# Interleaving two table-filling phases, spreading their pieces, and three smaller changes in an edge-gated graph kernel

## The chip, the cores and the metric

The kernel runs on one core of one Trainium2 chip. The metric is the device time of one execution in microseconds (us). A timed comparison alternates the changed kernel with the kernel before on the same chip. Chips differ: over the jobs of this study the kernel before had medians between 1218 and 1237 us. Kernels of different jobs are therefore compared by their ratio to the kernel before in the same job, not by their times. Unless a run is called slow, every run used here was in the fast state.

PE is the matmul engine (PEld its weight load), DVE the vector engine, ACT the scalar engine, POOL is GpSimd and SP the engine that issues most plain DMAs.

## The reference

There are 16 batches of 1024 nodes with 256 features. For each edge (u, v) of a sparse adjacency matrix, a small two-layer network gives a gate. The gated and the plain neighbour sums are then projected and added to the node:

```python
pre_u = einsum('bud,dk->buk', h_t, W1[:d])
pre_v = einsum('bvd,dk->bvk', h_t, W1[d:])
hidden = relu(pre_u[:, :, None, :] + pre_v[:, None, :, :] + b1)
S = sigmoid(einsum('buvk,ko->buvo', hidden, W2)[..., 0] + b2[0])
a_t = einsum('buv,bud->bvd', S * A_a, h_t)
m_t = einsum('uv,bud->bvd', A_m, h_t) * h_t
z_t = beta1*h_t + beta2*(einsum('bvd,de->bve', a_t, Wa) + ba) \
                + beta3*(einsum('bvd,de->bve', m_t, Wm) + bm)
```

The adjacency has about 0.9% of its entries set, so the kernel works on lists of edges instead of on all pairs.

## The kernel before

The batches form 4 groups of 4, the nodes 8 row blocks of 128. That makes 32 *blocks* (group, row block), each of ten *steps*. A step handles 128 edges: GpSimd gathers 128 rows of a table (`fetched`, one half x·W1-upper, the other half x), PE expands the target side of each edge (`pc`), DVE computes the gate, ACT the sigmoid and the weights (`left`), and PE aggregates into `acc`.

```python
def expand(n):                       # PE: target side of each edge of step n
    pcs[n] = psc.tile([P, GD], FP, name="pc")            # two buffers in PSUM
    for h in range(2):
        nc.tensor.matmul(pcs[n][:, c], marks[..], cuts[k][:, w, c], ...)
def gate(n):                         # DVE, then ACT
    nc.vector.tensor_tensor(t, fetched[..], pcs.pop(n), ALU.add)
    for b in range(GB):
        nc.vector.scalar_tensor_tensor(t[:, b, :], ..., accum_out=sc[:, b:b + 1])
    nc.scalar.activation(gt, sc, AF.Sigmoid, bias=b2_b)
    ...                              # left = one-hot x value x gate, on ACT
```

Beside this main line runs side work. `rows` fills a gather table ahead of need (products with `w_u`, in two halves per row block; all products of a half go into a buffer of the two-deep PSUM pool "misc"). `halves` prepares the next block's target side X (products with `w_v`; the rounding rest `low` is moved to the other 64 partitions by a swap matmul). `block_end` computes the output products, and `lists` makes the edge lists, on DVE above all.

```python
def rows(k, tab=None):
    for h in range(2):
        step = yield                                     # one piece per step
        half_product(p, hTs[k], w_u, h, False)           # 8 matmuls into "misc"
        nc.scalar.copy(tab[:, c], p)
def halves(k):
    ...                                                  # X[:, 0] and low, two pieces
    for h in range(2):
        yield
        nc.tensor.matmul(pl, swap, low[:, c], start=True, stop=True)
        for w in range(NW):
            s = slice((1 - w) * W, (2 - w) * W)
            nc.scalar.copy(X[s, w, c], pl[s])
# the main loop, cut
for n in range(total + 2):
    k, s = divmod(n, T)
    aggregate(n - 1); fetch(n - 1 + NF); gate(n)
    do(n)                                                # postponed DVE work, h_blk add too
    ...                                                  # s in 3..6: output products of block k-1
    if k + 1 < BS and s in (0, 2, 3, 4, 7): go(parts, n)     # a piece of halves
    if n in loads: load_hT(loads[n])                     # 512 KB of x transposed
    if n in at:    go(piece, n)                          # a piece of rows
    if n + 2 < total: expand(n + 2)
```

Groups 0 and 1 take turns every four row blocks, so that each edge list serves both. Their table pieces are packed tightly in the early blocks, and groups 2 and 3 have theirs in steps 8 and 9 of most blocks, with a cluster of group 3 in blocks 21 and 22.

## Time and profile before

| | kernel before |
|---|---|
| time, median of 3 runs | 1236.83 us (1234.14 to 1241.36) |
| span of the profiled run, mean granted clock | 1225.1 us, 0.964 |
| first gate starts at | 78.1 us |
| blocks 0 to 9 | 414.1 us |
| blocks 10 to 23 | 463.1 us, 33.1 a block |
| blocks 24 to 30 | 220.7 us, 31.5 a block |
| block 31 with the tail | 49.1 us |

The stretches are cut at the start of the gate's first DVE instruction in every tenth step, so they add up to the span. The profiled run was faster than all three timed ones. Differences between profiles therefore understate the change by several us against the timed runs, and the two sums below are not expected to agree.

Two more lines are needed later. These are ACT's instructions just before the first gate, from the timeline of the kernel before (start, us, engine, line, operation, tiles, shape, count, and in brackets the idle time before it and what ended it).

```profile
73.11 0.73 ACT L300 CAST few<-made 128x640 uint8<-128x640 f32 x1 [5.70 <-DVE made L294]
73.84 2.36 ACT L431 CAST X<-misc 64x512 fp32r<-64x512 f32 x4
76.10 0.72 ACT L523 CAST mark<-whose 128x640 fp32r<-128x640 uint8 x1
```

ACT took its instructions in the order of the program here. The four copies behind the swap matmuls (2.36 us) stand between the last list copy and the `mark` that the first expansion needs.

### The profile page before, as it was taken

What the parts mean: (1) busy time and instruction counts of PE and PEld (TensorE: products, weight loads), DVE (VectorE), ACT (ScalarE), POOL (GpSimd) and SP (SyncE); (2) the same over time, 40 slices, a digit from 0 to 9 for tenths busy, and PEclk for the clock granted to TensorE, in tenths of its full rate; (3) what the DMA queues carried; (4) which work ended last, traced back from release to release, by engine and by line L of the source; (5) the groups of instructions that cost most, each with busy time, mean ns of one, the idle gap of its engine ahead of it and who ended that gap; (6) DMA issues with size and microseconds to landing.
All of it is one profiled execution on the core that took longest, in us unless ns stands there. A gap on an engine that the chain in (4) does not pass through costs nothing. (4 is left out here: it accounts for less than half of the span.)

```text
span 1225.1 us, 23939 instructions
## 1 busy us (share of the span) xinstructions
PE 1110.8 (91%) x7697; PEld 723.6 (59%) x7697; DVE 1068.5 (87%) x3517; ACT 844.0 (69%) x2562; POOL 416.3 (34%) x412
## 2 busy tenths in 40 slices
PE   7665989988888988999999999999999999999986
PEld 6543666645555655666666556666666655665553
DVE  7667868898997889899999999998888999999994
ACT  2245567766666756778777777777777777887763
POOL 0345562326244314423233333332222333333330
PEclk9777999989898989999999999999999999999998
DMA  9688899977889979899999999999998998999992
GB/s 285 221 296 296 268 321 330 335 262 237 315 291 332 353 295 343 323 356 362 356 363 375 351 355 325 347 351 394 387 358 322 353 322 315 329 339 329 325 334 97
DMA packets 151975, 393.50 MB, mean 321 GB/s; under 512 B 16816, under 2 KB 110512, under 8 KB 115632
## 3 DMA queue, kind: packets, MB, share of 16 engines
q0 software_dynamic: 49504, 299.85, 66.5%
q1 hardware_dynamic: 85776, 77.08, 19.5%
q10 hardware_dynamic: 16560, 14.95, 3.8%
q8 instruction: 63, 1.03, 0.3%
q14 instruction: 72, 0.59, 0.1%
HBM read 395.88 MB, written 50.33 MB: 364 GB/s over the span
## 5 line engine op out<-in xcount | busy, mean ns | idle before, releaser
L459 POOL DMA_INDIRECT fetched<-table,uidx x320 | 326.7, 1021 | 717.1 <-PE acc L567 525.5
L550 DVE SCALAR_TENSOR_TENSOR t<-t,w_b 128x256 f32<-128x256 f32 x1280 | 469.6, 422 | 19.8
L546 DVE TENSOR_TENSOR t<-fetched,pc 128x1024 f32<-128x1024 f32 x320 | 389.2, 1216 | 68.9 <-PE pc L530 38.9
L567 PE MATMUL acc<-fetched,left 128*32 128x256 f32 x4096 | 323.4, 393 | 28.1 <-ACT left L556 21.9
L556 ACT ACTIVATE left<-left,gt 128x32 f32<-128x32 f32 (+1 forms) x1280 | 300.3, 306 | 10.4
L530 PE MATMUL pc<-X,mark 128*128 128x512 f32 x640 | 249.8, 472 | 5.4 <-ACT mark L523 5.4
L567 PEld LDWEIGHTS acc<-fetched,left 128*32 128x32 f32 x4096 | 121.3, 110 | 195.6 <-issue 71.6
L553 ACT ACTIVATE gt<-sc,b_b 128x4 f32<-128x4 f32 x320 | 95.5, 299 | 158.8 <-DVE t L550 150.7
L385 PE MATMUL misc<-w_u,hT 128*128 128x256 f32 x512 | 132.7, 407 | 19.8 <-ACT fetched L401 8.4
L530 PEld LDWEIGHTS pc<-X,mark 128*128 128x128 f32 x640 | 120.0, 195 | 29.8 <-ACT mark L523 5.9
L615 PE MATMUL misc<-w_m,LT 128*128 128x256 f32 x496 | 133.7, 392 | 0.0
L615 PE MATMUL misc<-w_a,LT 128*128 128x256 f32 x496 | 127.3, 379 | 0.0
L385 PEld LDWEIGHTS misc<-w_u,hT 128*128 128x128 f32 x512 | 99.3, 203 | 43.9 <-ACT fetched L401 8.9
L385 PE MATMUL misc<-w_v,hT 128*128 128x256 f32 x512 | 122.6, 383 | 0.0
L540 ACT ACTIVATE left<-onehot,val 128x128 f32<-128x128 bf16 (+1 forms) x320 | 117.5, 367 | 0.0
L615 PEld LDWEIGHTS misc<-w_m,LT 128*128 128x128 f32 x496 | 88.9, 189 | 34.8 <-issue 25.5
L385 PEld LDWEIGHTS misc<-w_v,hT 128*128 128x128 f32 x512 | 98.3, 192 | 13.2
L343 POOL DMA_INDIRECT val<-in_adjT_dram,vidx x80 | 85.3, 1066 | 60.9 <-DVE b_p L194 33.4
L550 DVE DVE_READ_ACCUMULATOR t<-t,w_b 128x1 f32 x1280 | 104.0, 81 | 0.0
L575 ACT COPY ev<-acc 128x512 f32<-128x512 f32 x128 | 74.9, 585 | 41.6 <-PE acc L567 28.6
L615 PEld LDWEIGHTS misc<-w_a,LT 128*128 128x128 f32 x496 | 94.2, 190 | 12.8
L585 PE MATMUL misc<-ident,ev 128*128 128x128 f32 x512 | 81.0, 289 | 15.8 <-DVE h_blk L619 8.5
(140 smaller groups left out, 820.3 us busy)
## 6 DMA issues: line engine op xcount, KB each, us to landing
hT<-in_xT_dram SPq DMA_DIRECT2D x40, 512.0 KB
h_blk<-in_x_dram SPq DMA_DIRECT2D x31, 512.0 KB
out_dram<-h_blk SPq DMA_DIRECT2D x31, 512.0 KB
table<-tab SPq DMA_DIRECT2D x26, 512.0 KB
table<-in_x_dram ACTq DMA_DIRECT2D x24, 512.0 KB
fetched<-table,uidx POOLq DMA_INDIRECT x320
table<-in_x_dram SPq DMA_DIRECT2D x8, 512.0 KB
table<-fetched SPq DMA_DIRECT2D x6, 512.0 KB
```

What stands on the lines that cost most here:

```text
L343: nc.gpsimd.indirect_dma_start(out=val[:, i, j:j + 1], out_offset=None, in_=adj_flat, in_offset=bass.IndirectOffsetOnAxis(ap=vidx[:, i, j: ...
L385: nc.tensor.matmul(p[:, bb * D:(bb + 1) * D], hT[:, 2 * h + bb, i, :], wt[:, i, :], start=(i == 0 and not begun), stop=(i == DC - 1), skip ...
L459: nc.gpsimd.indirect_dma_start(out=fetched[n % NF], out_offset=None, in_=table[g], in_offset=bass.IndirectOffsetOnAxis(ap=uidx[:, vt * NW ...
L530: nc.tensor.matmul(pcs[n][:, c], marks[n // TW][:, j * P:(j + 1) * P], cuts[k][:, w, c], start=True, stop=True)
L540: nc.scalar.activation(lefts[n][:, :m, :, 0, :], onehot[:, i, o:o + m, :].unsqueeze(2).to_broadcast([P, m, GB, V]), AF.Copy, scale=val[:, ...
L546: nc.vector.tensor_tensor(t, fetched[n % NF][:, :GD].rearrange("p (b d) -> p b d", b=GB), pcs.pop(n).rearrange("p (b d) -> p b d", b=GB), ...
L550: nc.vector.scalar_tensor_tensor(t[:, b, :], t[:, b, :], 0.0, w2_b, ALU.max, ALU.mult, accum_out=sc[:, b:b + 1])
L553: nc.scalar.activation(gt, sc, AF.Sigmoid, bias=b2_b)
L556: nc.scalar.activation(lefts[n][:, :m, b, 1, :], lefts[n][:, :m, b, 0, :], AF.Copy, scale=gt[:, b:b + 1])
L567: nc.tensor.matmul(accs[h][b * 2 * V:(b + 1) * 2 * V, r, :], left[:, i, b].rearrange("p k v -> p (k v)"), f[:, GD + b * D:GD + (b + 1) * D ...
L585: nc.tensor.transpose(pt[:, i * P:(i + 1) * P], ev[:, r, c * P:(c + 1) * P], ident)
L615: nc.tensor.matmul(pz[:, bb * D:(bb + 1) * D], LTs[k][:, c, 2 * h + bb, i, :], wt[:, c, :], start=False, stop=(i == 1 and c == DC - 1), sk ...
```

## The change

The intent is to interleave stretches bound by different engines, and to take waits and work off PE. The parts, with numbers used below: (a) the swap matmul goes, ACT copies `low` across the partitions itself. (b) The expansion for step n+2 comes right after the aggregation instead of at the end of the step. (c) Groups 0 and 1 take turns every six row blocks, and the `rows` pieces are spread evenly by `plan`. (d) GpSimd instead of ACT issues the small copies of the first four lists. With (c) come a new start-up script, an earlier fifth list, a pool of three for the reloaded x, and one buffer instead of two for the list tile `made`; no run separates these from the turns.

```diff
-        for h in range(2):
+        for w in range(NW):
             yield
-            c = slice(2 * h * D, (2 * h + 2) * D)
-            pl = small("pl")
-            nc.tensor.matmul(pl, swap, low[:, c], start=True, stop=True)
-            for w in range(NW):
-                s = slice((1 - w) * W, (2 - w) * W)
-                nc.scalar.copy(X[s, w, c], pl[s])
+            nc.scalar.copy(X[(1 - w) * W:(2 - w) * W, w, :], low[w * W:(w + 1) * W].bitcast(FP))
...
-                nc.scalar.dma_start(whose[...], few[...])
+                (nc.gpsimd if vt < EARLY else nc.scalar).dma_start(whose[...], few[...])
...
-    order = [(g, vt) for h in range(2) for g in range(2) for vt in range(h * NT // 2, (h + 1) * NT // 2)]
+    FIRST = 6
+    order = [(g, vt) for some in (range(FIRST), range(FIRST, NT)) for g in range(2) for vt in some]
...
-    at.update(zip((10 * i + s for i in range(7, 15) for s in (8, 9)), ((2, vt) ...)))
-    at.update(zip((178, 179, 188, 189, 198, 199, 208, 209, 211, 215, 217, 218, 219, 221, 228, 229), ((3, vt) ...)))
+    # plan: (load, first piece, second piece) in steps
+    plan(turn[NT:], ((0, 5, 8), (6, 12, 15), (12, 18, 22), (17, 25, 28), (24, 32, 35), (31, 38, 42), (38, 45, 48), (43, 50, 52)))
+    plan([(2, vt) ...], ((62 + 10 * i, 68 + 10 * i, 73 + 10 * i) for i in range(NT)))
+    plan([(3, vt) ...], ((146, 152, 157), (156, 162, 167), *((153 + 10 * i, 158 + 10 * i, 161 + 10 * i) for i in range(2, NT))))
+    plan(again, ((103,), (113,), (125,), (133,)))
...
         do(n)
+        if n + 2 < total:
+            expand(n + 2)
...
-        if k + 1 < BS and s in (0, 2, 3, 4, 7):
+        if k + 1 < BS and s in (0, 2, 3, 4, 6):
...
-        if n + 2 < total:
-            expand(n + 2)
```

More of the change, by code (lines that the diff above doesn't have):

```diff
@@ L178 @@
         nc.vector.tensor_scalar(slot_of[:, w, :], upto[:, :TW], float(P), row, ALU.mult, ALU.add)
-    swap = fixed([P, P], "swap", FR)
-    for w in range(NW):
-        nc.vector.tensor_scalar(swap[:, w * W:(w + 1) * W], upto[:, (1 - w) * W:(2 - w) * W], row, None, ALU.is_equal)
     ident = fixed([P, P], "ident")
@@ L216 @@
     hts = main.enter_context(tc.tile_pool(name="hts", bufs=NT + 2))
+    hta = main.enter_context(tc.tile_pool(name="hta", bufs=3))
     wk = main.enter_context(tc.tile_pool(name="wk", bufs=3))
@@ L288, in lists @@
         yield
-        mark = big.tile([P, E], FP, name="made")
+        mark = big.tile([P, E], FP, name="made", bufs=1)
         nc.vector.tensor_scalar(mark, slot, R[:, 0:1], None, ALU.is_lt)
@@ L305, in lists @@
             for h in range(2):
-                nc.scalar.dma_start(whose[h * W:(h + 1) * W, vt * NW + w, :], few[w * W:(w + 1) * W])
+                (nc.gpsimd if vt < EARLY else nc.scalar).dma_start(whose[h * W:(h + 1) * W, vt * NW + w, :], few[w * W:(w + 1) * W])
         pe = aside(vt)
@@ L361, in after @@
         due.setdefault(step, []).append(f)
-    order = [(g, vt) for h in range(2) for g in range(2) for vt in range(h * NT // 2, (h + 1) * NT // 2)]
-    again = [(g, vt) for g, vt in order if vt >= NT // 2]
+    FIRST = 6
+    order = [(g, vt) for some in (range(FIRST), range(FIRST, NT)) for g in range(2) for vt in some]
+    again = [(g, vt) for g, vt in order if vt >= FIRST]
     order += [(g, vt) for g in range(2, NG) for vt in range(NT)]
@@ L372, in load_hT @@
         g, nt = k
-        hTs[k] = hts.tile([P, GB, DC, P], FP, name="hT")
+        hTs[k] = hta.tile([P, GB, DC, P], FP, name="hT_") if k in again else hts.tile([P, GB, DC, P], FP, name="hT")
         nc.sync.dma_start(hTs[k].rearrange("p b c n -> p (b c) n"),
@@ L423, in halves @@
         nc.scalar.copy(X[W:, 1, :], X[W:, 0, :].bitcast(FP))
-        for h in range(2):
+        for w in range(NW):
             yield
-            c = slice(2 * h * D, (2 * h + 2) * D)
-            pl = small("pl")
-            nc.tensor.matmul(pl, swap, low[:, c], start=True, stop=True)
-            for w in range(NW):
-                s = slice((1 - w) * W, (2 - w) * W)
-                nc.scalar.copy(X[s, w, c], pl[s])
+            nc.scalar.copy(X[(1 - w) * W:(2 - w) * W, w, :], low[w * W:(w + 1) * W].bitcast(FP))
     engines = mybir.EngineType
@@ L465 @@
     made = [lists(vt) for vt in range(NT)]
-    turn = [order[i] for i in (*range(2 * NT // 2, 3 * NT // 2), *range(NT // 2))]
-    turn += [(1, vt) for _, vt in turn]
+    turn = [(g, vt) for g in range(2) for vt in (*range(FIRST, NT), *range(FIRST))]
     tabs = [fetched[0][:, :GD], *(f[:, GD:] for f in fetched)]
@@ L477 @@
         copy_h(turn[i], nc.sync)
-    script = ("r 0 0", "r r 0", "r 1", "0 r 1 1", "0 0 r r", "1 r 0 2 2", "r 0 0 v 2", "1 1 r r 2",
-              "r 1 r 3 3", "1 1 2 2 r h", "2 r r h 3", "2 2 3 h", "3 3 f h h")
+    script = ("r 0 0", "r r 0", "r 1", "0 r 1 1", "0 0 r r", "1 r 0 2 2", "r r 0 0 v 2", "1 1 r r",
+              "2 r 1 r", "2 2 r r 1 1 h", "2 h 3 3", "2 2 h 3", "f h h 3", "3 3")
     m = 0
@@ L666, with plan @@
     advance = {0: (3,), 2: (3,), 4: (3,)}
-    for i, n in zip(range(EARLY, NT), (0, 30, 50, 80)):
+    for i, n in zip(range(EARLY, NT), (0, 20, 50, 80)):
         for o in (0, 4, 5, 6, 7, 9, 11, 13, 15, 17):
             advance[n + o] = (*advance.get(n + o, ()), i)
-    loads = dict(zip((0, 1, 2, 6, 9, 13, 17, 23), turn[NT:]))
-    at = dict(zip((3, 5, 7, 8, 9, 11, 15, 17, 18, 19, 21, 25, 27, 28, 29, 31), (k for k in turn[NT:] for _ in range(2))))
-    loads.update(zip((58, 64, 66, 68, 70, 72, 93, 103), again))
-    loads.update(zip((74, 80, 86, 90, 113, 123, 133, 143), ((2, vt) for vt in range(NT))))
-    at.update(zip((10 * i + s for i in range(7, 15) for s in (8, 9)), ((2, vt) for vt in range(NT) for _ in range(2))))
-    loads.update(zip((173, 183, 193, 203, 206, 209, 214, 223), ((3, vt) for vt in range(NT))))
-    at.update(zip((178, 179, 188, 189, 198, 199, 208, 209, 211, 215, 217, 218, 219, 221, 228, 229),
-                  ((3, vt) for vt in range(NT) for _ in range(2))))
-    begun = set(turn)
+    loads, at = {}, {}
+    def plan(blocks, ns):
+        for k, (load, *pieces) in zip(blocks, ns):
+            loads[load] = k
+            at.update((n, k) for n in pieces)
+    plan(turn[NT:], ((0, 5, 8), (6, 12, 15), (12, 18, 22), (17, 25, 28), (24, 32, 35), (31, 38, 42), (38, 45, 48),
+                     (43, 50, 52)))
+    plan([(2, vt) for vt in range(NT)], ((62 + 10 * i, 68 + 10 * i, 73 + 10 * i) for i in range(NT)))
+    plan([(3, vt) for vt in range(NT)], ((146, 152, 157), (156, 162, 167), *((153 + 10 * i, 158 + 10 * i, 161 + 10 * i)
+                                                                             for i in range(2, NT))))
+    plan(again, ((103,), (113,), (125,), (133,)))
+    begun = set(turn[:NT])
     end = parts = piece = last = None
@@ L749 @@
             load_hT(loads[n])
-            if loads[n] not in begun or n < 30:
+            if loads[n] not in begun:
                 copy_h(loads[n])
+                begun.add(loads[n])
         if n in at:
```

## The prediction

> **What bounds the kernel now.** I read the page first: its busy shares and its slices, then the waits, then stretches of ten steps each. A step is one gather of 128 rows, its gate and its aggregation; ten make a block, and 32 blocks the kernel.
>
> ```profile
> PE 1110.8 (91%) x7697; PEld 723.6 (59%) x7697; DVE 1068.5 (87%) x3517; ACT 844.0 (69%) x2562; POOL 416.3 (34%) x412
> PE   7665989988888988999999999999999999999986
> DVE  7667868898997889899999999998888999999994
> PEclk9777999989898989999999999999999999999998
> ```
>
> PE and DVE are both nearly full, and neither is full all the time: the first 40% of the slices are thinner on both and have a lower granted clock, and in slices 28 to 31 DVE thins while PE does not. So one has to ask which is ahead in which stretch. The gate's first instruction (t<-fetched,pc) starts each step on DVE; I took its start times from the trace as the borders of the blocks. Here are blocks 0 to 4, 12, 21, 22 and 27. Columns: us, then busy us (instructions) of PE, weight load, DVE, ACT, POOL; granted clock; DMA share; GB/s.
>
> ```profile
> 78.10:131.30 53.20, 39.46 (x220) 25.80 (x220) 37.35 (x134) 26.64 (x81) 25.30 (x25) 0.77 0.86 295
> 131.30:175.00 43.70, 39.09 (x256) 27.16 (x258) 38.03 (x124) 27.47 (x80) 30.50 (x30) 1.00 0.96 318
> 175.00:215.10 40.10, 38.32 (x262) 26.01 (x266) 30.49 (x96) 27.46 (x83) 13.60 (x14) 1.00 0.94 326
> 215.10:256.70 41.60, 37.87 (x261) 24.02 (x261) 36.55 (x127) 28.48 (x88) 10.69 (x11) 0.88 0.85 301
> 256.70:295.00 38.30, 33.01 (x217) 20.39 (x216) 35.11 (x116) 24.14 (x73) 16.50 (x16) 0.96 0.83 284
> 557.00:589.50 32.50, 32.04 (x238) 21.00 (x234) 30.19 (x96) 25.70 (x80) 10.09 (x10) 1.00 0.97 366
> 850.20:887.90 37.70, 37.46 (x262) 25.61 (x261) 30.44 (x97) 27.49 (x84) 9.92 (x10) 1.00 1.02 379
> 887.90:921.90 34.00, 33.76 (x246) 22.56 (x247) 30.49 (x96) 26.33 (x81) 9.92 (x10) 1.00 0.99 357
> 1050.80:1081.90 31.10, 30.21 (x219) 18.88 (x218) 30.11 (x96) 24.64 (x78) 10.15 (x10) 1.00 0.90 325
> ```
>
> And blocks 2, 12 and 21 with w_u's instructions alone, PE and weight load only (x times W1's upper half, which fills the gather tables ahead of need):
>
> ```profile
> 175.00:215.10 40.10, 9.77 (x40) 7.27 (x40) 1.00 0.94 326
> 557.00:589.50 32.50, 3.89 (x16) 2.88 (x16) 1.00 0.97 366
> 850.20:887.90 37.70, 9.71 (x40) 7.27 (x40) 1.00 1.02 379
> ```
>
> What to see: a block without w_u and without list making takes 31.1 us and DVE works 30.1 of it: that is the floor, set by DVE. Eight w_u records are one half of a table's row block. A block with 2 halves takes 32.5, with 3 (x24) 34.0, with 5 (x40) 37.7; there PE has 0.2 to 0.5 us idle and DVE up to 7. The line through 2 and 5 halves is 29.05 + 1.73 per half, and gives 34.2 for 3. PE sets those blocks. Making the edge lists costs DVE about 6.4 and 5.0 us more in the two blocks that one list spans (36.5 and 35.1 against 30.1), and those blocks take 38 to 42.
>
> ```profile
> DVE t L546 <- PE pc L530: 38.9, 31, 5.7
> ACT X L431 <- PE misc L428: 20.2, 28, 1.5
> PEld misc L389 <- ACT X L431: 18.2, 23, 1.5
> PEld misc L428 <- ACT LT L588: 18.0, 24, 2.0
> DVE t L546 <- DMA fetched<-table,uidx: 11.5, 14, 2.4
> ```
>
> The gate waits for PE's expansion (pc), hardly for the gathers; and the swap matmul (L428) both waits for and holds up a buffer of the two-deep "misc" PSUM pool.
>
> **What the Trainium skill says.** "Perfetto Trace Analysis", section "Optimization Strategy": where the most-contended engine changes over time, interleaving the regimes can help. The blocks above are that case: PE-bound ones (5 halves) lie beside DVE-bound ones (none). "TensorE: Matmul & The Clock Gate", section "Wait — 56ns, not 53.3ns?": matmuls start N over 2.4 GHz plus about 2.5 ns apart, 215.7 ns for 512 columns. The trace differs: the 512-column fp32r swap holds its successor 0.42 us, the 256-column fp32 records start 0.216 us apart, so I take 0.42. Same page, "What's actually happening": an idle window halves the clock; here the clock is 0.77 in block 0 and 0.88 to 0.96 where PE idles 3 to 7 us of 40, so idle costs twice there. "DMA: Bandwidth & Descriptors", "Issuing engines are not separate DMA queues": another issuing queue saves only issue time. That bounds the copies moved from ACT to GpSimd: four ACT issues took 2.64 us at 47.3 us.
>
> **The change part by part.** (a) Swap removed. 64 matmuls go, 2 per block: 2 × 0.42 = 0.84 us of PE, and with them most of the wait at L389 and of those at the swap itself, (18.2 + 18.0) / 32 = 1.1 us per block on the weight-load side, of which I count half. PE per block: 29.05 − 1.4 = 27.65, plus 1.73 per half. ACT trades four copies of 0.58 (2.33) for two of 64x1024, which L423 shows to take 1.05 (2.09): no gain worth counting. With 2 halves PE then needs 31.1, just DVE's floor; with 3 it needs 32.8.
> (b) Expansion of step n+2 right after the aggregation, ahead of the side work. PE does the same work, but the pc waits (38.9 us, of which three steps of block 0 have 12.8) should nearly go from the other blocks. This makes it possible to reach the floor; I do not count it twice.
> (c) Turns of six blocks and even spreading. From the schedule, halves per block before: 5, 5, 5, 1 in blocks 0 to 3; 2 each in 7 to 14 and in 17 to 20, then 5 and 3 in 21 and 22. After: 2, 3, 3, 3, 3, 2 in blocks 0 to 5; about 2 in 7 to 13; 2 or 1 in 15 to 23. Four instead of eight 512 KB reloads of x transposed go too: 2 MB of 393, hidden.
> (d) 16 small list copies to GpSimd, 10.6 us of ACT issue in the start-up, where ACT is half idle.
>
> Sum. Blocks 10 to 23 took 463.1 us (492.2 to 955.3). PE and DVE now both stand at 31.1, so I take 31.3: 14 × 31.3 = 438.2, gain 25. Blocks 24 to 30 took 220.7; 7 × 31.2 = 218.4, gain 2. Early blocks, 0 to 9, took 414.1. Block 0: three halves fewer by plan, cold clock, 53.2 to 48. Block 1: 43.7 to 40.5 (DVE 38 plus 2.5 of waits). Blocks 2 and 3: list 5 moves in by ten steps beside 3 halves; 81.7 to 78.5. Block 4: no list now, 3 halves on PE, 38.3 to 34. Blocks 5 to 9, list-bound: 197.2 to 192. Together 393, gain 21. Start-up before the first gate (78.1) and tail (49.1): the same chains; 0. Total 48, so 1237 − 48 = 1189; two for gathers that come under pressure at a faster pace: 1191.
>
> **The rivals.** First, gathers become the bound. For: DMA share 0.97 to 1.02 in the w_u blocks; block 12's 366 GB/s over 32.5 us would become 380 at 31.3. Against: block 21 ran at 379 with share 1.02 and its gates waited for PE, not DMA; all gather waits are 11.5 us. If true, blocks 10 to 23 stay near 32.3: 14 us of gain lost, 1205. Second, the early expansion stalls PE: it needs the buffer that gate n empties, and where 2 to 4 us of list work stand ahead of that gate on DVE, PE waits instead of doing side work. For: blocks 3 to 9 have such list work. Against: PE has slack there and side work is needed a step later. If true, early gain shrinks to about 5: 1207. Third, DVE's floor is the bound everywhere and the clustering was already paid inside PE slack: then only blocks 18 to 23 and block 0 gain, 1215. Fourth, the moved copies stand ahead of the first gathers on GpSimd and delay the start by 3 to 8 us.
>
> **Range and chances.** The late gain (18 to 30) is read from a fitted line, the early one (5 to 35) is rough, start-up ±5. In the middle 1191, eighty per cent within 1172 to 1213. The 2% limit is 1212, so faster 0.86, same 0.13, slower 0.01.
>
> **What would show it.** Blocks 10 to 30 should all take 31 to 31.6 us, DVE busy 30.1, PE busy under it; no L428; pc waits under 15 us; blocks 1 to 4 between 34 and 41. Gates waiting over 30 us for gathers would show the first rival; PE waits for DVE t before pc the second; a first gate after 82 us the fourth. Blocks of 32.5 with 2 halves would disprove (a).

## The result, and the profile after

| | before | after |
|---|---|---|
| median, 4 runs each | 1235.49 us (1232.73 to 1241.36) | 1198.01 us (1196.87 to 1204.65) |
| ratio of fast runs, 95% interval | | 0.9702 (0.965 to 0.9753): faster |
| profiled span, clock | 1225.1 us, 0.964 | 1195.2 us, 0.973 |

A ratio here is the mean time of one kernel's fast runs over that of the other's fast runs of the same rounds, so it is not quite the ratio of the medians. The change gains 37 us; 46 were predicted. By stretches of the two profiles:

| stretch | before | after | gain | predicted gain |
|---|---|---|---|---|
| start to the first gate | 78.1 | 68.5 | 9.6 | 0 |
| block 0 | 53.2 | 43.8 | 9.4 | 5 |
| blocks 1 to 9 | 360.9 | 352.1 | 8.8 | 16 |
| blocks 10 to 23 | 463.1 | 463.3 | −0.2 | 25 |
| blocks 24 to 30 | 220.7 | 217.8 | 2.9 | 2 |
| block 31 and tail | 49.1 | 49.6 | −0.5 | 0 |

The total came out near, but its parts did not: more than half of the expected gain was to come from blocks 10 to 23, and there came none. From the page of the kernel after (busy shares, then two rows of the 40 slices, in tenths):

```profile
PE 1097.9 (92%) x7633; PEld 724.7 (61%) x7633; DVE 1066.9 (89%) x3515; ACT 840.4 (70%) x2498; POOL 426.1 (36%) x428
DVE  8769879989988988899899999999999999999994
PEclk9968899999999999999999999999999999999998
```

The thin DVE slices 28 to 31 of before are gone, and the clock drops only in a few early slices. PE ran 64 matmuls fewer, as it should. Now blocks 0, 3, 12, 13, 21 and 27 of the kernel after (columns as in the prediction's table of blocks):

```profile
68.54:112.33 43.79, 35.33 (x214) 21.92 (x213) 37.29 (x133) 25.91 (x78) 28.00 (x28) 0.79 0.80 252
198.05:236.14 38.09, 36.22 (x264) 24.90 (x256) 34.97 (x118) 26.71 (x79) 16.30 (x16) 1.00 0.89 316
532.72:565.69 32.97, 32.63 (x234) 21.74 (x235) 30.28 (x96) 25.81 (x78) 10.48 (x11) 1.00 0.98 363
565.69:601.42 35.73, 33.48 (x233) 21.66 (x231) 30.29 (x97) 25.70 (x78) 10.61 (x10) 0.95 0.97 358
830.78:862.76 31.98, 31.41 (x229) 20.52 (x227) 30.29 (x96) 25.68 (x78) 9.74 (x10) 1.00 1.00 363
1021.10:1052.21 31.11, 29.97 (x218) 19.01 (x216) 30.12 (x97) 24.57 (x76) 10.21 (x11) 1.00 0.93 329
```

Block 27 is at the floor of 31.1, as predicted. Block 21 no longer carries five halves: 37.7 became 32.0. But block 12, an ordinary block with two halves, took 32.97 where it had taken 32.50, with PE still at 32.63, although its swap matmuls are gone. Block 13 was longer still, with a clock of 0.95. The waits of the kernel after that answer to those shown of before (us in total, times, longest):

```profile
DVE h_blk L612 <- PE misc L608: 20.6, 21, 2.7
DVE low L419 <- ACT X L418: 19.7, 16, 4.4
DVE t L539 <- DMA fetched<-table,uidx: 8.6, 14, 1.2
DVE t L539 <- PE pc L523: 3.4, 3, 2.0
```

The gate's wait for PE's expansion fell from 38.9 to 3.4 us, and all waits at the swap are gone. In their place DVE waits 20.6 us for the output products (`h_blk`, once 1.3) before it can add them. This wait stands in front of the next gate on DVE's queue. ACT at the start, from the timeline of the kernel after:

```profile
65.87 0.72 ACT L298 CAST few<-made 128x640 uint8<-128x640 f32 x1 [7.03 <-DVE made L292]
66.50 0.72 ACT L516 CAST mark<-whose 128x640 fp32r<-128x640 uint8 x1
```

The last list copy came 7.2 us earlier (73.11 to 65.87), and `mark` followed it at once instead of after 2.36 us of swap copies; together that is the 9.6 us.

Block 13's loss has another cause. These are one matmul group on PE and the issue of the load that it needs:

```profile
551.09 0.65 SPq L373 DMA_DIRECT2D hT__6071<-in_xT_dram  x1
...
570.69 3.26 PE L384 MATMUL misc<-w_v,hT__6071 128*128 128x256 f32 x8 [2.25 <-DMA hT__6071<-in_xT_dram]
```

The 512 KB load was issued five steps before the w_v product that needs it and took 19.5 us to land (at 570.64). PE stood still for 2.25 us, and the granted clock was at half for the next 3.4 us: these eight matmuls took 3.26 us instead of 1.89.

### The profile page after: what moved, and what is told of

It reads as the page before. It is cut to its first block, busy times and chain, and to the rows that moved or that the text cites. A ratio compares the mean times of both kernels' runs of the same rounds, so it can differ in the third digit from the quotient of the medians.

```text
span 1195.2 us, 23788 instructions
## 1 busy us (share of the span) xinstructions
PE 1097.9 (92%) x7633; PEld 724.7 (61%) x7633; DVE 1066.9 (89%) x3515; ACT 840.4 (70%) x2498; POOL 426.1 (36%) x428
## 3 DMA queue, kind: packets, MB, share of 16 engines
q0 software_dynamic: 50016, 300.50, 68.5%
## 5 line engine op out<-in xcount | busy, mean ns | idle before, releaser
L539 DVE TENSOR_TENSOR t<-fetched,pc 128x1024 f32<-128x1024 f32 x320 | 388.8, 1215 | 22.4 <-DMA fetched<-table,uidx 8.6
L560 PE MATMUL acc<-fetched,left 128*32 128x256 f32 x4096 | 334.2, 394 | 32.3 <-ACT left L549 16.8
L523 PE MATMUL pc<-X,mark 128*128 128x512 f32 x640 | 238.1, 454 | 21.1 <-DVE t L539 13.6
L560 PEld LDWEIGHTS acc<-fetched,left 128*32 128x32 f32 x4096 | 129.9, 110 | 177.2 <-issue 46.9
L523 PEld LDWEIGHTS pc<-X,mark 128*128 128x128 f32 x640 | 97.2, 191 | 156.6 <-issue 102.2
L608 PE MATMUL misc<-w_m,LT 128*128 128x256 f32 x496 | 127.1, 378 | 0.0
L384 PE MATMUL misc<-w_u,hT 128*128 128x256 f32 x448 | 109.2, 390 | 11.0 <-ACT few L298 3.6
L384 PE MATMUL misc<-w_v,hT 128*128 128x256 f32 x448 | 107.9, 384 | 0.0
L384 PEld LDWEIGHTS misc<-w_u,hT 128*128 128x128 f32 x448 | 85.8, 195 | 27.3 <-issue 4.4
L384 PEld LDWEIGHTS misc<-w_v,hT 128*128 128x128 f32 x448 | 86.7, 194 | 14.3
L581 ACT COPY LT<-misc 128x512 f32<-128x512 f32 x128 | 71.1, 575 | 24.0 <-PE pc L523 12.0
```

The lines of the kernel that those rows point to most:

```text
L384: nc.tensor.matmul(p[:, bb * D:(bb + 1) * D], hT[:, 2 * h + bb, i, :], wt[:, i, :], start=(i == 0 and not begun), stop=(i == DC - 1), skip ...
L523: nc.tensor.matmul(pcs[n][:, c], marks[n // TW][:, j * P:(j + 1) * P], cuts[k][:, w, c], start=True, stop=True)
L539: nc.vector.tensor_tensor(t, fetched[n % NF][:, :GD].rearrange("p (b d) -> p b d", b=GB), pcs.pop(n).rearrange("p (b d) -> p b d", b=GB), ...
L560: nc.tensor.matmul(accs[h][b * 2 * V:(b + 1) * 2 * V, r, :], left[:, i, b].rearrange("p k v -> p (k v)"), f[:, GD + b * D:GD + (b + 1) * D ...
L608: nc.tensor.matmul(pz[:, bb * D:(bb + 1) * D], LTs[k][:, c, 2 * h + bb, i, :], wt[:, c, :], start=False, stop=(i == 1 and c == DC - 1), sk ...
```

## The experiments

Twelve kernels ran, in four jobs on four chips; all gave correct results. To compare blocks 10 to 23, the length of the stretch and PE's busy time in it are given each time. PE's busy time holds stalls inside a stream of matmuls too, so it is read as "the PE sequence got longer", not as pure work.

### First job: which of the parts

**late_expand**: the kernel after, with the expansion back at the end of the step.

```diff
         do(n)
-        if n + 2 < total:
-            expand(n + 2)
...
             go(piece, n)
+        if n + 2 < total:
+            expand(n + 2)
```

> The changed kernel with one edit: the expansion of step n+2 goes back to the end of the step. Theory 'order of neighbours': in the changed trace a step's matmul groups cost PE 0.309 (side work to aggregation) + 0.309 (aggregation to expansion) + 0.337 + 0.231 = 1.19 us of start-to-start time beside their own rows, in the old order 0.028 + 0.418 + 0.327 + 0.309 = 1.08, so 0.10 us a step or 1.0 us a block is given back in the PE-bound blocks. Then blocks 11 to 23 fall from 32 to 33 us to about 31.3, blocks 24 to 30 rise from 31.1 to about 31.4, and the whole gets 8 to 12 us faster than the changed kernel (about 1188). Rival 'pc waits': the late expansion is what made the gate wait for pc (38.9 us before, little now); then the waits return and the whole gets 5 to 12 us slower (about 1207).

**three_small**: the kernel before with (a), (b) and (d), without the turns and the spreading.

> The kernel before with the three small changes only: no swap matmul, expansion early in the step, list copies of the first four lists issued by GpSimd; old turns, old start-up script, old loads. Theory: the early expansion gives back in PE-bound blocks what the swap's removal gains there, so two-half blocks stay at 32 to 32.5; blocks 24 to 30 reach 31.1; start-up gains a few us from the copies. 10 to 15 us under before, about 1222; then turns and spreading are worth the other 24. Rival: the small changes are the gain and the turns nothing: about 1200.

**before_early**: the kernel before with (b) alone.

```diff
         do(n)
+        if n + 2 < total:
+            expand(n + 2)
...
-        if n + 2 < total:
-            expand(n + 2)
```

> The kernel before with the early expansion alone. 'Order of neighbours' says: PE-bound blocks 10 to 22 get about 1 us slower each (33.5 with two halves), DVE-bound blocks 24 to 30 get 0.3 faster, the early blocks lose their pc waits: within 10 us of before, more likely slower, 1235 to 1245. 'Pc waits' says 10 to 20 us faster, 1215 to 1225.

**keep_swap**: the kernel after with the swap matmul put back.

```diff
-            nc.scalar.copy(X[(1 - w) * W:(2 - w) * W, w, :], low[w * W:(w + 1) * W].bitcast(FP))
+            pl = small("pl")
+            nc.tensor.matmul(pl, swap, low[:, c], start=True, stop=True)
+            ...   # and the four copies, pieces in steps 0, 2, 3, 4, 7
```

> The changed kernel with the swap matmul put back (64 matmuls, their PSUM buffers and four half copies a block). If the swap cost PE 0.8 us a block plus half of the waits around it, as the prediction counted (1.4), the PE-bound blocks 7 to 23 and 0 to 5 rise by that: 20 to 30 us slower than the changed kernel, about 1222. If it cost only its own 0.4 us each where PE is the bound: about 12 to 16 slower, 1212. If DVE is the bound everywhere: 0 to 3.

| run | median (before: 1232.62, 15 runs) | ratio, 95% | blocks 0 to 9 | blocks 10 to 23 | PE busy in these |
|---|---|---|---|---|---|
| late_expand | 1200.42, 4 runs | 0.9734 (0.9659 to 0.9809) | 394.3 | 462.5 | 445.5 |
| three_small | 1212.03, 4 runs | 0.9839 (0.9769 to 0.991) | 404.9 | 462.8 | 451.9 |
| before_early | 1234.68, 12 runs | 1.0027 (0.9987 to 1.0068) | 413.9 | 467.5 | 460.5 |
| keep_swap | 1210.64, 4 runs | 0.9824 (0.9755 to 0.9893) | 405.5 | 462.0 | 454.4 |

The early expansion by itself gives nothing. It does what it was made for: the gate's waits for the expansion fell from 38.9 to 8.4 us. But blocks 10 to 23 became longer and PE busier. One line for that stretch of the kernel before, then the same of before_early:

```profile
492.20:955.34 463.14, 452.19 (x3263) 295.26 (x3261) 423.79 (x1348) 358.52 (x1103) 144.53 (x144) 1.00 0.97 355
```

```profile
491.15:958.66 467.51, 460.53 (x3289) 298.99 (x3288) 424.67 (x1347) 359.94 (x1107) 143.73 (x144) 1.00 0.96 352
```

PE does the same matmuls, 8.3 us longer. The starts of successive matmuls in blocks 11 to 19 and 24 to 30 show why: what a matmul costs its successor depends on the neighbours. Before, a step has the borders side work to expansion (median 0.028 us), expansion to expansion (0.418), expansion to aggregation (0.327) and aggregation to side work (0.310): 1.08 us. With the early expansion they are aggregation to expansion (0.309), expansion to expansion (0.337), expansion to side work (0.232) and side work to aggregation (0.309): 1.19 us. That is 0.10 us per step or 1.0 us per block if PE is the bound. The median of eight ordinary blocks (11 to 15 and 18 to 20) went from 32.7 to 33.2, so about half of it shows. This is what the theory "order of neighbours" had expected, a run within 10 us of before. The side work also comes later, and DVE's waits move to what hangs on it.

keep_swap against the kernel after shows (a) to be real: ratio 0.9824 against 0.9702, with intervals that just do not overlap. That is about 1.2% or 15 us, the middle case of the expectation (the swap's own 0.4 us each) and not the 20 to 30 us that 1.4 us a block would give. In blocks 10 to 23 the two profiles are alike: 462.0 and 463.3 us. three_small, 20 us under before by its ratio, fell between its theory (10 to 15) and its rival. late_expand missed both theories, between the two. PE's busy time fell by 7.3 us against the kernel after (452.8 to 445.5), as the neighbours say, but the stretch stayed at 462.5, because a new wait took the gain. The wait list of blocks 10 to 23 has this line for late_expand, against 2.7 us in the kernel after:

```profile
PEld misc L384 <- DVE low L419: 8.8, 6, 2.4
```

A w_u piece placed one step after a w_v piece wants the "misc" buffer that DVE's `low` has not read yet; this was in blocks 18 to 23, where the piece lies in step 1. three_small, finally, has ordinary blocks at 31.8 to 32.0 with one exception, where the kernel after has 32.0 to 33.2 and block 13 with 35.7. So something in the spreading makes ordinary blocks slower.

### Second job: what in the spreading

**pieces_89**: the kernel after, with the pieces of groups 2 and 3 back in steps 8 and 9 of their blocks, still spread over the blocks.

```diff
-    plan([(2, vt) ...], ((62 + 10 * i, 68 + 10 * i, 73 + 10 * i) ...))
-    plan([(3, vt) ...], ((146, 152, 157), (156, 162, 167), *((153 + 10 * i, 158 + 10 * i, 161 + 10 * i) ...)))
+    plan([(2, vt) ...], ((62 + 10 * i, 68 + 10 * i, 69 + 10 * i) ...))
+    plan([(3, vt) ...], ((146, 158, 159), (156, 168, 169), *((153 + 10 * i, 158 + 10 * i, 159 + 10 * i) ...)))
```

> The changed kernel with the two w_u pieces of a block in its steps 8 and 9 again, as before the change, instead of 8 and 3 (or 2 and 7, 8 and 1); the same number per block, the same loads. Theory 'lumps': in steps 3 to 6 PE already has the output products, and a piece there makes DVE wait for them (the h_blk additions waited 20.6 us for PE in the changed kernel, 1.3 before), the gate comes late and PE then waits at the aggregation. With the pieces at 8 and 9 the h_blk waits fall under 6 us and blocks 11, 12 and 14 to 22 fall from 32 to 33.5 to the 31.8 that the kernel with the three small changes shows with two pieces: 8 to 10 us faster than the changed kernel, about 1189. Rival: spread pieces are better for PE, and the blocks stay or rise: 0 to 5 us slower.

**early_loads**: the kernel after, with the loads of x transposed of group 2 and three of the four reloads 8 or 10 steps earlier.

```diff
-    ... ((62 + 10 * i, 68 + 10 * i, 73 + 10 * i) ...)
-    plan(again, ((103,), (113,), (125,), (133,)))
+    ... ((54 + 10 * i, 68 + 10 * i, 73 + 10 * i) ...)
+    plan(again, ((95,), (105,), (115,), (133,)))
```

> The changed kernel with the loads of x transposed for the second part of groups 0 and 1 and for group 2 issued 8 to 10 steps earlier, pieces unmoved. Theory: PE waited 2.4 us at 459.6 and 2.7 us at 570.7 for such a load, after which the clock fell to half for 3.4 us each; blocks 9, 10 and 13 (42.2, 35.6, 35.7) fall by about 2.5 each: 6 to 8 us faster than the changed kernel, about 1191. Rival: the loads are slow because the DMA engines are full, and come late anywhere: no change.

**both_moves**: both edits.

> Both: pieces at steps 8 and 9 and the earlier loads. If the two causes are separate their gains add: 14 to 18 us faster than the changed kernel, about 1182, blocks 10 to 23 in sum 445 to 450 against 463. If they are one (the load waits only happen because PE is thrown off), the gain is that of the better one alone.

**before_noswap**: the kernel before with (a) alone.

> The kernel before without the swap matmul, nothing else changed: old turns, late expansion. From the PE sequence of block 12 (swap to expansion 0.75, transposes to swap 0.51 us, the shorter second expansion matmul behind it 2 x 0.19 given back, and part of the evictions' waits) the two-half blocks should fall from 32.5 to about 31.5, under the 31.8 that they take with the early expansion. In all 10 to 16 us under before, about 1220. If the swap hid in PE waits instead: no change.

| run | median (before: 1234.8, 7 runs) | ratio, 95% | blocks 0 to 9 | blocks 10 to 23 | PE busy in these |
|---|---|---|---|---|---|
| pieces_89 | 1195.26, 4 runs (one slow, 1211.1) | 0.9667 (0.9613 to 0.9721) | 404.7 | 450.6 | 445.2 |
| early_loads | 1204.97, 4 runs | 0.976 (0.9715 to 0.9805) | 401.8 | 462.9 | 452.6 |
| both_moves | 1194.46, 4 runs | 0.9673 (0.9616 to 0.9731) | 399.6 | 455.9 | 447.4 |
| before_noswap | 1215.16, 4 runs | 0.9842 (0.9797 to 0.9886) | 407.7 | 460.3 | 447.9 |

pieces_89 tests the middle: the same early part up to step 68, the same order and the same matmuls, but 12.7 us less in blocks 10 to 23. First the mechanism in the kernel after, PE's timeline in block 12 (lines left out), then the DVE instruction that waits:

```profile
546.95 1.89 PE L384 MATMUL misc<-w_u,hT 128*128 128x256 f32 x8
548.77 1.07 PE L560 MATMUL acc<-fetched,left 128*32 128x256 f32 x16
...
550.34 1.02 PE L608 MATMUL misc<-w_m,LT 128*128 128x256 f32 x4
551.21 1.03 PE L608 MATMUL misc<-w_a,LT 128*128 128x256 f32 x4
```

```profile
552.27 0.75 DVE L612 SCALAR_TENSOR_TENSOR h_blk<-h_blk,be,misc 128x512 f32<-128x512 f32 x1 [1.28 <-PE misc L608]
```

And the same place of pieces_89:

```profile
554.75 1.07 PE L560 MATMUL acc<-fetched,left 128*32 128x256 f32 x16
...
556.32 1.02 PE L608 MATMUL misc<-w_m,LT 128*128 128x256 f32 x4
557.18 1.03 PE L608 MATMUL misc<-w_a,LT 128*128 128x256 f32 x4
```

```profile
559.13 0.74 DVE L612 SCALAR_TENSOR_TENSOR h_blk<-h_blk,be,misc 128x512 f32<-128x512 f32 x1
```

Steps 3 and 4 of a block are PE's fullest: the output products of the block before lie there. The kernel after puts a w_u piece of 1.9 us into step 3 as well. PE then ends the second set of output products at 552.2, when DVE has already stood for 1.28 us. The next gate comes behind this addition on DVE, at 552.94, and so starts late. Without the piece in step 3 PE has ended at 558.2 and DVE comes at 559.13 without a wait. In blocks 10 to 23, the wait list has these lines for three_small and for the kernel after (and none at all for pieces_89):

```profile
DVE h_blk L611 <- PE misc L607: 1.1, 2, 0.8
```

```profile
DVE h_blk L612 <- PE misc L608: 10.3, 13, 2.0
```

So 13 of the 14 blocks had it, and its size goes with the place of the piece. In blocks 10 to 17 (a piece in step 3 up to block 14, in step 2 in blocks 15 and 16) the waits come to 8.8 us and pieces_89 gains 11.4, with the same number of halves; 3.3 of these lie in block 13, where the load came almost in time in its profile. In blocks 18 to 23 (piece in step 1) the waits come to 1.5 us and the gain to 1.3.

The wait at `h_blk` is not the only form that this cost takes. late_expand has the pieces in the same steps as the kernel after, and waits in blocks 10 to 23 like this:

```profile
DVE t L539 <- PE pc L523: 9.3, 25, 0.9
DVE h_blk L612 <- PE misc L608: 2.1, 13, 0.2
```

There the gate waits for PE's expansion instead, and the stretch is as long (462.5). Moving the pieces to steps 8 and 9 with the expansion late (late_expand to mixed, of the third job) shortens blocks 10 to 17 by 6.9 us, on another chip. On one chip, early_loads and both_moves differ in the pieces alone, and the stretch fell from 462.9 to 455.9. So the place of the piece costs time under both orders, and the order of the expansion decides where DVE waits.

In the whole run the gain of pieces_89 is small (0.9667 against 0.9702, intervals overlapping; 8 to 10 us were expected). Its profile lost 8.8 us again in blocks 0 to 9 against the kernel after (404.7 to 395.9). The two programs are the same up to step 68, and 6.3 us of the difference lie in blocks 1 to 6, so most of this is scatter between runs and chips. It is also the limit of what single profiles can say about the early part.

early_loads missed. Block 13 came down from 35.7 to 32.6 us, but other waits appeared, such as one of 2.6 us at 831.84 for a load of group 3, which has the same lead of five steps and was not moved. Whether the earlier loads pushed this one back was not tested. (The wait at 459.6 that the expectation names is not put down to a load by the trace.) Both moves together gave no more than pieces_89 alone.

before_noswap settles (a) in the whole run: ratio 0.9842. Of the same eight ordinary blocks two (12 and 20) waited for a load of x in this profile; the median of the others fell by 0.6 (32.7 to 32.1; 31.5 was expected). With the early expansion on both sides (before_early to three_small) the median of the eight fell by 1.3 (33.2 to 31.9). With the spread pieces on both sides (keep_swap to the kernel after) it fell by 0.2 (33.1 to 32.8). With the swap gone, adding the early expansion and (d) (three_small) brings nothing in the whole run, and PE is 4.0 us busier in the stretch (447.9 to 451.9).

### Third job: the turns alone, the start, and a mixture

**turns_only**: the kernel before with (c) alone, that is, the kernel after with (a), (b) and (d) undone.

> The kernel before with turns of six, the new start-up script and the new loads and pieces alone: swap kept, late expansion, list copies issued by ACT. The three small changes alone gave 0.984 of before. If the parts add, turns alone give 0.970 / 0.984 = 0.986 of before, about 1217, with blocks 0 to 9 about 10 us shorter and blocks 10 to 23 no better than before (the two clustered blocks 21 and 22 gain 8, the two-half blocks lose as much by the piece beside the output products). Rival: turns are worth what I forecast (c) to give, 25 us or more, and the small changes overlap with them: 1205.

**copies_act**: the kernel after, with ACT issuing the list copies again, as before.

```diff
-                (nc.gpsimd if vt < EARLY else nc.scalar).dma_start(whose[...], few[...])
+                nc.scalar.dma_start(whose[...], few[...])
```

> The changed kernel with the list copies of the first four lists issued by ACT again. Theory: their issue time stands in ACT's in-order queue before the evictions that the start-up waits for; the kernels with GpSimd issue have their first gate at 68.5 to 73.1 us, those with ACT issue at 77.3 to 79.2. First gate 5 to 7 us later, about 75, and the whole 5 to 8 us slower than the changed kernel, about 1205. Rival: the earlier first gate comes from the new script: no change.

**mixed**: pieces_89, with the expansion late up to step 230 and early from there on, where no table is filled any more.

```diff
+        # with the pieces in steps 8 and 9
-        if n + 2 < total:
+        if n >= 230 and n + 2 < total:
             expand(n + 2)
...
+        if n < 230 and n + 2 < total:
+            expand(n + 2)
```

> The changed kernel with the w_u pieces at steps 8 and 9, and the expansion late in the step while there are w_u pieces (to step 229), early after. From the PE sequences: two-half blocks at 31.5 (late, no swap, pieces together) instead of 31.8 (early) and 32 to 33.5 (changed kernel); blocks 24 to 30 at 31.1. Blocks 10 to 23 in sum about 445, the whole about 1188, 0.992 of the changed kernel, the fastest of all. Rival: the late expansion brings the pc waits back and the two-half blocks stay at 32 or above.

| run | median (before: 1218.42, 11 runs) | ratio, 95% | first gate | block 0 | blocks 1 to 9 | blocks 10 to 23 |
|---|---|---|---|---|---|---|
| turns_only | 1199.31, 4 runs | 0.9833 (0.9804 to 0.9863) | 76.7 | 43.2 | 342.2 | 466.1 |
| copies_act | 1185.72, 4 runs | 0.9737 (0.9701 to 0.9772) | 75.0 | 42.8 | 340.4 | 458.9 |
| mixed | 1171.02, 6 runs | 0.9617 (0.9586 to 0.9647) | 71.1 | 41.0 | 338.1 | 462.8 |

This chip is faster by some 15 us for the kernel before, and copies_act, which differs from the kernel after only in who issues 16 small copies, took 340.4 us in blocks 1 to 9 instead of 352.1. The difference of the chips therefore seems to lie in the early blocks; only ratios, and the block borders common to many runs, may be compared.

Those borders are clear in two places. Over the whole study, block 0 takes 40.9 to 44.2 us in all ten kernels that have the turns of six and 48.5 to 53.2 in all four that have not. The first gate comes at 68.5 to 73.1 us where GpSimd issues the list copies and at 75.0 to 79.2 where ACT does. Three pairs of kernels agree on the way: DVE's wait in the start-up for ACT's copy to `L` (`s_of` in the wait lists) is 3.3 to 3.5 us shorter with GpSimd issuing (before to three_small 10.2 to 6.7, copies_act to the kernel after 4.7 to 1.4, turns_only to keep_swap 6.5 to 3.0; only the second pair differs in nothing else). In the whole run the copies are worth at most a little: 0.9737 against 0.9702, which the intervals do not separate.

turns_only came nearer to its theory (0.986) than to its rival of 1205, with 0.9833. mixed was the fastest so far, as expected, but blocks 10 to 23 took 462.8 us in its profile where 445 were expected. The profiled run of mixed was its slowest (1182.87, the other five 1167.57 to 1178.56). PE waited for a load of x transposed four times, once for 6.62 us. This is its line in the list of PE's waits:

```profile
PE misc L384 <- DMA hT<-in_xT_dram: 14.4, 4, 6.6
```

All four are loads of group 3 with a lead of five steps.

### Fourth job: a longer lead

**mixed_loads**: mixed, with the loads of group 3 eighteen steps ahead instead of five; three of them go into the pool of three buffers.

```diff
-    ... *((153 + 10 * i, 158 + 10 * i, 159 + 10 * i) ...)
+    ... *((140 + 10 * i, 158 + 10 * i, 159 + 10 * i) ...)
-        hTs[k] = hta.tile(...) if k in again else hts.tile(...)
+        hTs[k] = hta.tile(...) if k in again or k in ((3, 2), (3, 3), (3, 4)) else hts.tile(...)
```

> The mixed kernel (pieces at steps 8 and 9, expansion late to step 229) with the loads of x transposed for group 3 issued 18 steps ahead of their first piece instead of 5, three of them in the idle buffers of the second pool. In the trace of mixed PE waited 7.1, 2.7, 3.4 and 3.0 us for just these loads, four waits of 16 us in blocks 18 to 21, and in the kernels with the same 5-step lead 1 to 5 us there. If the lead is the cause these waits vanish, blocks 18 to 22 fall to 31.5 to 32, blocks 10 to 23 to about 446 in sum, and the ratio to before goes from mixed's 0.962 to about 0.952. If loads come late at random whatever the lead, waits of the same size stay and the ratio too.

Measured: 1169.81 us, 6 runs (1164.46 to 1174.39), beside 1219.53 for the kernel before (11 runs): ratio 0.9594 (0.9563 to 0.9625). That misses the expectation of more, but it is the fastest version of the study, and its interval is clear of the kernel after's (0.965 to 0.9753), as mixed's just is. The stretch of blocks 10 to 23:

```profile
449.73:899.41 449.68, 440.55 (x3225) 288.06 (x3223) 423.80 (x1347) 354.53 (x1076) 149.00 (x146) 1.00 1.00 371
```

PE's busy time is the lowest of all, no group-3 load is waited for any more, and there is no wait at `h_blk`. The block mean is 32.1 us all the same. The gates of this stretch now wait 10.1 us in all for their gathers (7.2 before, 6.0 after), 0.7 a block, at a DMA share of 1.00: this is the first rival of the prediction, met late and on a small scale. Against mixed the interval does not separate (0.9586 to 0.9647), so the longer lead shows in the waits and not yet in the time. How often mixed's other runs had its load waits is not known, as only the slowest was profiled. That the late expansion does better than the early one in this setting is likewise only indicated, by 4.6 us less PE busy time than in pieces_89; the stretches are as long, 449.7 and 450.6.

## Why the prediction was right or wrong

**The whole**: 1191 predicted, 1198 measured, within the range, and rightly called faster by over 2%. The nearness of the total is in part luck: 25 us failed to come in blocks 10 to 23 and 7 in blocks 1 to 9, and 14 came that were not forecast, 9.6 in the start and 4 in block 0.

**(a) The swap: right in direction, too large in size.** The step "27.65, plus 1.73 per half" meant 1.4 us less per ordinary block. They fell by 1.3 in one pair of kernels, by 0.6 from the kernel before and by 0.2 in the kernel after; PE's busy time in blocks 10 to 23 fell by 8.7, 4.3 and 1.6 us in these pairs, where 14 × 1.4 = 20 were counted. The whole run fell by 1.6%. The prediction said that blocks of 32.5 with two halves would disprove it. Such blocks appeared and it was right nevertheless; the test was badly chosen, as it could not tell (a) from a loss elsewhere.

**(b) The early expansion: the step that failed is "PE does the same work".** The matmuls are the same, the sequence is not: 1.19 instead of 1.08 us per step for the four borders, 2.8 to 8.3 us more PE busy time in blocks 10 to 23 over four pairs of kernels (before_early over before, three_small over before_noswap, which differ in (d) too, the kernel after over late_expand, pieces_89 over mixed). The waits fell as said, from 38.9 to 3.4 us, but no gain shows in the whole run: 1.0027 alone.

**(c) Blocks 10 to 23: "PE and DVE now both stand at 31.1, so I take 31.3".** This is the step that failed: 25 us predicted, none measured. DVE was busy 30.3 us a block, near the 30.1 that were said, but PE 32.3 before and after (452.2 and 452.8 over 14 blocks), not 31.1. By the pairs of kernels, what (a) took off, (b) and the places of the pieces put back. The place of work within a block was not considered: a piece in step 3 delays the output products, DVE waits for them 10.3 us in 13 blocks, and moving the pieces to steps 8 and 9 gives 12.7 us back, with 7.6 us less PE busy time. The clusters in blocks 21 and 22 did go, by 6.8 us together (37.7 + 34.0 to 32.0 + 32.9), but blocks 10 and 13 lost as much (32.0 + 33.2 to 35.6 + 35.7). In block 13 that was a load that came late; in block 10 the granted clock was at half for 3.4 us from 472.27, for a reason that was not found. Of the 25 us, about half is there to be had, as pieces_89 and mixed_loads show at 450; the rest was not found, and the gathers hold part of it.

**(c) The early blocks: 21 predicted for blocks 0 to 9, 18 in the profiles.** The direction of block 0 was right and its size was not: 9.4 instead of 5. The turns give 10.0 to 11.7 there with the expansion late (before to turns_only, before_noswap to late_expand) and 4.7 to 4.9 with it early (three_small to the kernel after, before_early to keep_swap; two of the four pairs differ in (d) too). Blocks 1 and 2 came out at 43.4 and 42.3, over the 41 that the prediction named as the limit. Blocks 1 to 9 gave 8.8 instead of 16, but single profiles scatter by about as much there, so nothing is concluded from it.

**(d) and the start: "the same chains; 0" was wrong, with 9.6 us.** The copies on ACT stood in the way of the last list, and the swap copies ahead of the first expansion. The prediction knew the issue time (10.6 us for 16; 12 of them, 7.2 us, come before the first gate) and let it go because ACT is half idle in the start-up. But DVE waits there for a copy that ACT makes after its issues, and GpSimd's issuing shortened that wait by 3.3 us (copies_act to the kernel after). The first gate came 6.4 us earlier in this pair; how much of that is scatter is not known, since the nine kernels with GpSimd's issuing spread over 4.6 us. The fourth rival, a start delayed by the copies on GpSimd, did not occur.

**(c) and (a) carry the change.** Alone, (a) has a ratio of 0.9842 and (c) 0.9833. Their product is 0.968, and the whole change has 0.9702. So (b) and (d) together add nothing that these runs can see. This multiplies ratios of two chips and is no measurement by itself.

**The other rivals.** Gathers did not become the bound of the kernel after: its gates waited 8.6 us for them, less than before (11.5). The second rival, PE waiting for the gate before an expansion, is there but small: 13.6 us on PE in the whole run. The third, that DVE's floor is the bound everywhere, is refuted by before_noswap, where the swap went, DVE's work stayed (424.1 us busy in blocks 10 to 23 against 423.8), and the run got shorter all the same. That its 1215 is just what turns_only's ratio gives on the kernel before (0.9833 × 1235.5) is chance: its gains were to lie in block 0 and blocks 18 to 23, and blocks 10 to 23 of turns_only are 3 us longer than before. One reading of the clock was too simple: 0.88 to 0.96 was said to go with 3 to 7 us of idle PE, but block 1 has 4.6 us of it at 1.00. Blocks 24 to 30 were right in size, 217.8 against 218.4.

**Left open**: what holds ordinary blocks of the best version at 32 instead of 31.3 beyond the 0.7 us of gather waits, and how much of the early blocks' gain belongs to which part.

## What to carry to other kernels

When work is spread over the steps of a pipeline, balancing the sum per period is not enough: keep a piece out of the steps in which the same engine has results due that another engine waits for, and look at that engine's wait list after every move. Moving an instruction on an engine can change the cost of all its neighbours, so time the sequence and not the instruction. Issue prefetches with a lead that fits the busiest DMA stretch, not the mean one.

## What the Trainium skill lacked or had wrong

- "TensorE: Matmul & The Clock Gate", "Wait — 56ns, not 53.3ns?" gives one spacing per column count at full clock. In this kernel 256-column fp32 matmuls started 0.216 us apart, and two 512-column fp32r expansions 0.337 or 0.418 us, according to what stood before them. No page has a cost by neighbours: 0.028 us from side work to an expansion, 0.309 from an aggregation to one, 0.327 from an expansion to an aggregation, which came to 1.08 or 1.19 us per step for the same matmuls.
- "DMA: Bandwidth & Descriptors", "Issuing engines are not separate DMA queues" says that another issuer saves only issue time, usually small beside the DMA itself. It does not say what that time costs the other work of the issuing engine. Here it mattered: a start-up wait of DVE for ACT was 1.4 instead of 4.7 us, and the first gate came at 68.5 to 73.1 us with GpSimd issuing the list copies and at 75.0 to 79.2 with ACT.
- No page has the time that a plain load needs while gathers fill the DMA engines: 512 KB took 19.5 us from issue to landing at a DMA share of 0.98, and a lead of five steps (some 16 us) was not enough.
